# A fused attention kernel: layer 1's merged values by two levels of Strassen instead of one

## The chip, the core and the metric

The kernel runs on one core of a Trainium2 chip. A core has a matrix engine (TensorE, PE in the profile, with its weight loads shown as PEld), a vector engine (VectorE, DVE), an activation engine (ScalarE, ACT), GpSimd (POOL) and SyncE (SP); the last two issue the kernel's DMAs. Operands live in SBUF, TensorE writes to PSUM. The metric is the device time of the whole program in microseconds (us); less is better.

## What is computed

The input is x of shape (8, 512, 32, 32) in fp32: eight batches of 1024 tokens with 512 channels. Two layers follow each other. All of it is in fp32.

```python
# layer 0, per batch
xn = layer_norm(x_flat)                       # over channels
q, k, v = xn @ Wq.T + bq, xn @ Wk.T + bk, xn @ Wv.T + bv     # 8 heads of 64
attn = softmax(q @ k.T / sqrt(64)); out = attn @ v
x = out @ Wo.T + bo + x_flat
# layer 1, per batch, one head of 512 channels
h = group_norm(x, 32 groups)
q, k, v = wq @ h + bq, wk @ h + bk, wv @ h + bv
attn = softmax(q.T @ k / sqrt(512)); o = v @ attn.T
x = x + wp @ o + bp
```

In layer 1 the kernel folds matrices that follow each other into one. The value projection and the output projection become one matrix `m` (wp times wv), so that the "merged values" are m times h, and attention times merged values is already the layer's output. The merged values, 1024 tokens by 512 channels from 512 channels, are the part that is changed.

## The kernel before

**Strassen products.** Almost every matrix product is cut into 2 x 2 blocks and made by Strassen's scheme in Winograd's form: seven products of half-size blocks in place of eight. The list `STEPS` gives the order. Step 0 multiplies block 11 of the weight by block 11 of the operand, step 1 12 by 21, step 2 the sums S2 and T2, step 3 S1 and T1, step 4 S3 and T3, step 5 S4 and 22, step 6 22 and T4. S sums are made of weight blocks (for the merged values they were saved to DRAM once and are loaded with the blocks), T sums of operand blocks. Steps accumulate into three PSUM banks x, z and y. Between the steps ScalarE copies an intermediate state of a bank out (u1, u2, u4 in `leave`, by `plain_shift`) and VectorE adds a copy and a bank into the result (`out`, line 386). The class `Product` holds such a chain: `multiply` issues the matmuls of one step, `leave` the copies and sums that follow it.

**Two levels.** Some products go one level deeper: the half-size products are made by the same seven steps of quarter-size blocks. Two products that end in the same sum run "in tandem", accumulating into the same banks (`project_mixed` for layer 1's queries, `project_deep` for the next batch's keys and queries). The inner sums of weights come from DRAM (`saved_deep`, `load_deep`), the inner sums of operands are "primes", made by VectorE. The queries of layer 1, `project_mixed`, leave the primes of T1, T2, T3 and 22 of h in the dictionary `h1_deep`, and they stay in SBUF through the scores.

**The order within a batch.** For each batch: layer 0's heads (scores, softmax, values), output projection, group norm, layer 1's queries (`project_mixed`), scores (`Whole.scores`, three pairs of products), then the stage in question: the merged values (`project_v(f"vm{b}", ...)`), then the layer's output (`Whole.values`, tiles named o, the units `o_units`), then the next batch's keys and queries (`project_deep`). TensorE, ScalarE, VectorE and GpSimd run in the order in which the program issues (the `manual_schedule` blocks). Work that is not urgent goes into a queue `side` by `later(...)`. `tick(n)` takes n pieces from its front, and the calls of `tick` are spread by hand over the matmul steps (`pieces`). At the merged values this queue holds the end of layer 1's scores (sums `p<-p,p`, line 1360, exponentials, line 1308), the denominator's sums (line 1412) and the operand sums T1 to T4 of the attention weights (line 1423).

**The merged values before.** `project_v` makes two units, one for each half of the tokens of a block. Each runs the seven steps; each step is four matmuls (two token blocks of 128, two halves of the contraction) with 128 stationary columns (operand h) and 256 moving columns (the weight), by `token_part` (line 490). Each unit has four ScalarE copies of 128x512 and three VectorE sums of 128x512. A result `vm` of 1024 tokens is laid out with the token block outermost.

**The output stage.** The units of `Whole.values` run by `value_part` (line 506): four matmuls of 512 moving columns for each step. Before, they run as: two steps of unit 0, two of unit 1, then the rest of unit 0 with some of unit 1, then the rest of unit 1. The weight sums S1 to S4 of the merged values (line 268) are made by VectorE from `later` queue pieces during this stage. `LayerNorm` of the batch after next also puts its pieces there (`ln.queue()`).

**Buffers.** The pool `big` has 46 tiles of 128x1024 fp32, used in rotation by everything of that size; a DMA into a tile on SyncE's queue waits until the former content's last reader is done, and the DMAs behind it wait too. PSUM has three 128x1024 tiles (`wide_psum`) and two of 128x512 (`bank`).

Of the kernel before, what the change touches and what calls it, by code (L numbers as in the profile page):

```python
# [71 lines left out]
def fast_path(ctx: ExitStack, tc: tile.TileContext, x: bass.AP, vecs: dict, weights: dict, out: bass.AP,  # L72
# [48 lines left out]
    def wide(blk):  # L121
        return blk.rearrange("p a t -> p (a t)")
# [89 lines left out]
    saved_deep = {n: dram.tile([P, 3, 2, 4, P], F32, tag=f"saved_deep_{n}", name=f"saved_deep_{n}") for n in ("k", "q", "a")}  # L212
# [289 lines left out]
    def value_part(r):  # L502

        def part(dst, a, b, opens):
            for m in range(NM // 2):
                nc.tensor.matmul(dst, a[:, m, ts(r, P)], b[m // 2][:, m % 2, :], start=(opens and m == 0),  # L506
                                 stop=(m == NM // 2 - 1), skip_group_check=True)
        return part
# [179 lines left out]
    def project_mixed(tag, w, w_deep, bias, h, primes, between, away, beside, ready):  # L688
# [121 lines left out]
        return {(1, 0): m6}, closing  # L810

# [451 lines left out]
    class Whole:  # L1263
# [204 lines left out]
        def values(self, v):  # L1468
            b = self.b
            more = b + 1 < B  # L1470
            w = {f"{i + 1}{j + 1}": v[i, j].rearrange("p (m o) -> p m o", o=CB) for i in range(2) for j in range(2)}
            shared = {}

            def unit(r):
# [25 lines left out]
                def halves(u):  # L1500
# [9 lines left out]
                    for cols in both:  # L1510
                        for m in range(NM // 2):
                            nc.tensor.matmul(u.x[:, cols], w[a][:, m, ts(r, P)],
                                             self.p[b_][m // 2][:, m % 2, cols], start=False,
                                             stop=(m == NM // 2 - 1), skip_group_check=True)
# [12 lines left out]
            for n in SUM_NAMES:  # L1527
                sum_later(w, n, lambda n: big_tile(f"{n}_vm_{b}").rearrange("p (m o) -> p m o", o=CB), wide)
# [18 lines left out]
    with tc.manual_schedule(engines=ORDERED):  # L1547
# [66 lines left out]
        save_deep_later("a", wa, (1, 2))  # L1614
        units, vts = project_v("v0", wv_now, hb)
# [5 lines left out]
        for b in range(B):  # L1621
# [144 lines left out]
            wm_now = load_w("m", b)  # L1766
            next(steps)
            next(steps)
            whole.operands("T2", "T3", "T4")
            v_units, vm = project_v(f"vm{b}", wm_now, h1b)  # L1770
            for u, pieces in zip(v_units, ((2, 2, 2, 2, 1, 1, 1), (1, 1, 1, 2, 1, 2, 2))):
                for u.pieces in pieces:
                    u.step(1)
# [6 lines left out]
            o_units[0].step(2)  # L1780
            if ln:
                ln.queue()
            o_units[1].step(2)
# [20 lines left out]
            if more:  # L1804
                h_deep = {}
                deep_operands_later(hb, h_deep, [n for _, names in TANDEMS for n in names])
# [401 lines left out]
```

## Time and profile before

| | |
|---|---|
| median of 3 runs | 2800.3 us (2799.87 to 2800.49) |
| the profiled execution, its own time | 2798.97 us |
| its span (first to last instruction) | 2797.2 us |
| VectorE busy | 2095.1 us (75%) |
| ScalarE busy | 1248.2 us (45%) |
| GpSimd busy | 527.6 us (19%) |
| HBM read, written | 198.21 MB, 63.44 MB |
| granted clock of TensorE | 1.000 (mean) |

The profile is one execution seen by the hardware's profiler. Groups of instructions are shown as line, engine, operation, output <- inputs with buffer numbers left out, shape, count | busy time, mean duration in ns | idle time of the engine just before them. Each fp32 matmul of the program appears as two records, each with its own weight load: the 56 matmuls that make one batch's merged values stand as 112 records, 896 for the eight batches. Busy time of overlapping records is not counted twice. The start of the merged values of the eight batches lies at 348.1, 689.2, 1030.3, 1371.6, 1712.7, 2053.8, 2394.8 and 2718.4 us. The third, at 1030.27 us, is the one looked at closely.

### The profile page before, as it was taken

Reading aid. Unit: us, or ns where it says so; the run is one execution under the profiler, and the core shown is the slowest. Engines: PE = TensorE matmul, PEld = TensorE weight load, DVE = VectorE, ACT = ScalarE, POOL = GpSimd, SP = SyncE. Lnnn points to the kernel's source line nnn. Section 1 sums busy time; section 2 is a strip of 40 time slices with the busy share of each in tenths; the row PEclk is TensorE's granted clock in tenths of the full one; section 3 lists DMA queues with packets and bytes.
Section 4 is the critical chain, followed back from the end, with each engine's and each line's share of the span. In section 5 each row is a group of like instructions: output and inputs, shape, how many; then the busy total and the mean of one; then the engine's idle time right before and its main releaser. Section 6 shows DMA issues by size and latency. Waiting matters only on the chain.

```text
span 2797.2 us, 31704 instructions
## 1 busy us (share of the span) xinstructions
PE 2786.4 (100%) x10959; PEld 1625.5 (58%) x10959; DVE 2095.1 (75%) x2978; ACT 1248.2 (45%) x2114; POOL 527.6 (19%) x724
## 2 busy tenths in 40 slices
PE   9999999999999999999999999999999999999999
PEld 4535756358553685536854467644676347663375
DVE  6677877778777777777867777678867778657775
ACT  4463425724257242662436533365334733336341
POOL 2031022210222102221122211222112210122001
PEclk9999999999999999999999999999999999999999
DMA  8244367353763547536474364744548433382224
GB/s 318 92 97 125 110 163 191 68 151 110 166 164 70 169 107 181 129 78 188 108 183 107 91 184 108 201 79 117 151 113 208 101 95 117 71 208 63 66 79 99
DMA packets 141018, 365.56 MB, mean 131 GB/s; under 512 B 19776, under 2 KB 24176, under 8 KB 140848
## 3 DMA queue, kind: packets, MB, share of 16 engines
q0 software_dynamic: 58992, 144.22, 27.7%
q1 hardware_dynamic: 81760, 219.19, 22.7%
q8 instruction: 89, 1.46, 0.2%
q14 instruction: 81, 0.66, 0.1%
q10 hardware_dynamic: 96, 0.02, 0.0%
HBM read 198.21 MB, written 63.44 MB: 94 GB/s over the span
## 4 chain that ended last, share of the span: by engine, by line
PE 99%; DMA 0%; DVE 0%; ACT 0%; issue 0%; SPq 0%; DVEq 0%
PE s L1154 16%; PE acc L1172 16%; PE x_o L506 8%; PE s L1320 7%; PE x_v L490 4%; PE x_vm L490 4%; PE y_o L506 4%; PE x_out L481 4%; PE y_s L1320 3%; PE y_v L490 2%; PE y_vm L490 2%; PE s L1355 2%; PE y_out L481 2%; PE z_o L506 2%; PE x_q L604 2%; PE x_k L604 2%
## 5 line engine op out<-in xcount | busy, mean ns | idle before, releaser
L1163 DVE TENSOR_TENSOR sum<-sum,p 128x1024 f32<-128x1024 f32 x384 | 470.3, 1225 | 39.4 <-DVE sum L1163 0.9
L1157 ACT ACTIVATE p<-s 128x1024 f32<-128x1024 f32 (+1 forms) x608 | 478.8, 992 | 15.1 <-PE s L1154 15.1
L1172 PE MATMUL acc<-p,v_again 128*64 128x512 f32 x1792 | 390.9, 594 | 0.0
L1172 PEld LDWEIGHTS acc<-p,v_again 128*64 128x64 f32 x1792 | 126.1, 137 | 261.4 <-issue 236.7
L861 POOL DMA_DIRECT2D fold<-sum x312 | 207.7, 760 | 301.8 <-DMA sum<-sum 174.8
L1154 PE MATMUL s<-q,k 64*128 64x512 f32 x1152 | 252.1, 592 | 0.0
L1154 PE MATMUL s<-q_lower,k_lower 64*128 64x512 f32 x896 | 196.1, 592 | 0.0
L1161 DVE TENSOR_TENSOR sum<-p,p 128x1024 f32<-128x1024 f32 x64 | 78.1, 1220 | 153.0 <-ACT p L1157 153.0
L1154 PEld LDWEIGHTS s<-q,k 64*128 64x128 f32 x1152 | 109.7, 186 | 138.2 <-issue 84.9
L1154 PEld LDWEIGHTS s<-q_lower,k_lower 64*128 64x128 f32 x896 | 85.4, 186 | 110.5 <-issue 68.5
L865 POOL DMA_DIRECT2D sum<-sum x78 | 63.5, 814 | 456.2 <-DVE sum L1163 253.1
L1176 ACT COPY o<-acc 128x512 f32<-128x512 f32 x63 | 36.9, 585 | 221.7 <-PE acc L1172 221.5
L1360 DVE TENSOR_TENSOR p<-p,p 128x1024 f32<-128x1024 f32 x96 | 114.1, 1215 | 6.3 <-ACT p L511 6.3
L506 PE MATMUL x_o<-T_p,S_vm 128*128 128x512 f32 x256 | 114.0, 592 | 0.0
L511 ACT COPY u(0, 0)_v<-x_v 128x512 f32<-128x512 f32 x16 | 9.4, 585 | 186.5 <-PE x_v L490 186.5
L1416 POOL DMA_DIRECT2D sum<-p x32 | 28.0, 925 | 334.6 <-ACT p L1308 240.8
L490 PE MATMUL x_vm<-w_m,T_gn 128*128 128x256 f32 x384 | 90.7, 379 | 0.0
L481 PE MATMUL x_out<-T_o,w_o 128*128 128x512 f32 x192 | 89.2, 594 | 0.0
L506 PEld LDWEIGHTS x_o<-T_p,S_vm 128*128 128x128 f32 x256 | 48.6, 190 | 60.7 <-issue 60.5
L1218 ACT COPY rr<-r 32x16 f32<-32x16 f32 x256 | 53.7, 210 | 62.0 <-DVE r L1121 58.6
L490 PE MATMUL x_v<-w_v,T_h 128*128 128x256 f32 x336 | 80.0, 381 | 0.0
L490 PEld LDWEIGHTS x_vm<-w_m,T_gn 128*128 128x128 f32 x384 | 72.9, 190 | 10.0
(621 smaller groups left out, 5455.7 us busy)
## 6 DMA issues: line engine op xcount, KB each, us to landing
sum<-sum POOLq DMA_DIRECT2D x78, 256.0 KB, 3.4
fold<-sum POOLq DMA_DIRECT2D x312, 64.0 KB, 2.4
x<-in_x_dram SPq DMA_DIRECT2D x32, 512.0 KB, 4.7
xr<-in_x_dram SPq DMA_DIRECT2D x64, 256.0 KB, 4.7
x_away<-x SPq DMA_DIRECT2D x32, 512.0 KB, 3.2
sum<-p POOLq DMA_DIRECT2D x32, 512.0 KB, 5.8
v_away<-v SPq DMA_DIRECT2D x28, 512.0 KB
v_again<-v_away SPq DMA_DIRECT2D x28, 512.0 KB, 7.9
```

The lines of the kernel that those rows point to most:

```text
L481: nc.tensor.matmul(dst, a[:, k, ts(r, P)], b[:, k, :], start=(opens and k == 0), stop=(k == 1), skip_group_check=True)
L490: nc.tensor.matmul(dst[:, ts(m, CB)], b[:, k, ts(2 * r + m, P)], a[:, k, :], start=(opens and m == 0 and k == 0), stop=(k == 1), skip_grou ...
L506: nc.tensor.matmul(dst, a[:, m, ts(r, P)], b[m // 2][:, m % 2, :], start=(opens and m == 0), stop=(m == NM // 2 - 1), skip_group_check=True)
L604: nc.tensor.matmul(dst[:, ts(s, CB)], a[s], b[s], start=(opens and s == 0), stop=True, skip_group_check=True)
L861: nc.gpsimd.dma_start(out=f[ts(q + i, BL), :], in_=t[ts(n, BL), ts(i, HB)], accum_op=ALU.add if n else ALU.bypass)
L1154: nc.tensor.matmul(parts[i], self.k[m // 4][r, ts(m % 4, P)], self.q[r, :], start=True, stop=True)
L1157: nc.scalar.activation(dst, src, AF.Exp, scale=1.0 / float(D) ** 0.5)
L1161: nc.vector.tensor_add(self.sum, self.p[0], p)
L1163: nc.vector.tensor_add(self.sum, self.sum, p)
L1172: nc.tensor.matmul(acc[i * D : (i + 1) * D, :], value_of(self.vt, m, self.c * P + i * D, D), self.p[m][:, ts(i, HB)], start=(m == 0), stop ...
L1320: nc.tensor.matmul(dst[:, ts(c, CB)], x[0][:, ts(c, P)], a[0], start=(opens and c == 0), stop=True, skip_group_check=True)
L1360: nc.vector.tensor_add(wide(t), wide(t), wide(x))
```

## The change

The merged values are made by a new function, `project_values`. Three of Strassen's seven outer products (m1 = 11 by 11, m2 = 12 by 21, m6 = 22 by T4) are made whole: eight matmuls of 256 moving columns each, into the three wide PSUM tiles, and copied out by ScalarE (`evict`, 128x1024). The other four run as two tandems by a second level: unit B takes (S2 by T2) and (S3 by T3), unit C takes (S1 by T1) and (S4 by 22). Each unit has seven inner steps of four matmuls with 128 stationary and 128 moving columns. The inner operand sums are those that the queries left in `h1_deep`; the inner weight sums are saved once at the start (`save_deep_later("m", ...)`, eight small VectorE sums and two DMAs) and loaded for each batch (`load_deep("m", b, (1, 2))`, two DMAs of 512 KB on SyncE's queue, right after the four of the blocks and in front of the next x). The outer results are then put together: m2 += m1 by an accumulating DMA on GpSimd's queue, and twelve VectorE sums of 128x512 (`add` in `project_values`), some of them in the `side` queue.

The results are laid out with the channel half outermost, so `value_part` and the last batch's `halves` read them by `a[:, r, ts(m, P)]`. The sums T3 and T4 of the attention weights are queued behind S2 and S4 of the merged values (in `Whole.values`), and so in the output stage, whose units take their pieces as 5, 1 and 3, 2. The first two of the next batch's inner operands (11 and T2 of h) are made earlier in the output stage, from the same stage's queue.

```diff
--- before.py
+++ after.py
@@ -209,7 +209,7 @@
             nc.sync.dma_start(out=t, in_=d)
         return w
 
-    saved_deep = {n: dram.tile([P, 3, 2, 4, P], F32, tag=f"saved_deep_{n}", name=f"saved_deep_{n}") for n in ("k", "q", "a")}
+    saved_deep = {n: dram.tile([P, 3, 2, 4, P], F32, tag=f"saved_deep_{n}", name=f"saved_deep_{n}") for n in ("k", "q", "a", "m")}
 
     def deep_tile(n, b, g):
         return big_tile(f"w_{n}_{b}_{g}_deep").rearrange("p (s i o) -> p s i o", s=2, i=4)
@@ -503,7 +503,7 @@
 
         def part(dst, a, b, opens):
             for m in range(NM // 2):
-                nc.tensor.matmul(dst, a[:, m, ts(r, P)], b[m // 2][:, m % 2, :], start=(opens and m == 0),
+                nc.tensor.matmul(dst, a[:, r, ts(m, P)], b[m // 2][:, m % 2, :], start=(opens and m == 0),
                                  stop=(m == NM // 2 - 1), skip_group_check=True)
         return part
 
@@ -809,6 +809,112 @@
         q21, q22 = (block(f"{tag}_{n}") for n in ("21", "22"))
         return {(1, 0): m6}, closing
 
+    def project_values(tag, w, w_deep, h, deep):
+
+
+        n_blocks = {n: block(f"{tag}_{n}") for n in ("m1", "m2", "m6")}
+        banks = {n: wide_psum(f"{n}_{tag}") for n in "cba"}
+        made = [[None, None], [None, None]]
+
+        def products(n, t, pairs):
+            a, x = {"m1": ("11", "11"), "m2": ("12", "21"), "m6": ("22", "T4")}[n]
+            for r in pairs:
+                for m in range(2):
+                    for k in range(2):
+                        nc.tensor.matmul(banks[t][:, r * HB + m * CB : r * HB + (m + 1) * CB], h[x][:, k, ts(2 * r + m, P)],
+                                         w[a][:, k, :], start=(k == 0 and m == 0), stop=(k == 1),
+                                         skip_group_check=True)
+
+        def evict(n, t):
+            nc.scalar.copy(n_blocks[n].rearrange("p r (m o) -> p r m o", o=P),
+                           banks[t].rearrange("p (m r o) -> p r m o", r=2, o=P))
+
+        def part(dst, a, x, opens):
+            for s in range(2):
+                for m in range(2):
+                    nc.tensor.matmul(dst[:, ts(2 * s + m, P)], x[s][:, ts(m, P)], a[s],
+                                     start=(opens and s == 0 and m == 0), stop=True, skip_group_check=True)
+
+        def unit(j):
+            def dest(i, k):
+                if made[j][i] is None:
+                    made[j][i] = big_tile(f"{tag}_{j}{i}").rearrange("p (s t) -> p s t", s=2)
+                return made[j][i][:, :, ts(k, CB)]
+
+            def bank_of(to):
+                if to == "y":
+                    return bank(f"y_{tag}_{j}")
+                return banks["c"][:, ts(j, HB)] if to == "z" else banks["ab"[j]][:, :HB]
+
+            a, x = ((("S2", "S3"), ("T2", "T3")), (("S1", "S4"), ("T1", "22")))[j]
+            u = Product(f"{tag}_{j}", weight_inner(w, w_deep, a), operand_inner(h, deep, x), part, plain_shift,
+                        dest, bank_of)
+            u.view = lambda t: t.rearrange("p (s t) -> p s t", s=2)
+            return u
+
+        def step(u, n=1):
+            u.multiply()
+            tick(n)
+            u.leave()
+
+        def add(dst, l, src):
+            nc.vector.tensor_add(dst, l, src)
+
+        def both(work):
+            for r in range(2):
+                work(r)
+
+        m1, m2, m6 = (n_blocks[n] for n in ("m1", "m2", "m6"))
+        products("m1", "c", (0, 1))
+        tick(2)
+        evict("m1", "c")
+        B, C_ = unit(0), unit(1)
+        products("m2", "b", (0, 1))
+        tick(2)
+        evict("m2", "b")
+        step(B)
+        step(B)
+        nc.gpsimd.dma_start(out=wide(m2), in_=wide(m1), accum_op=ALU.add)
+        step(B)
+        step(C_)
+        step(B)
+        step(C_)
+        step(B)
+        step(C_)
+        step(B)
+        products("m6", "c", (0,))
+        tick(1)
+        step(B)
+        step(C_)
+        mb, mc = made
+        both(lambda r: add(mb[r][:, 0], mb[r][:, 0], m1[:, r]))
+        step(C_)
+        products("m6", "c", (1,))
+        both(lambda r: add(mb[r][:, 1], mb[r][:, 1], mb[r][:, 0]))
+        evict("m6", "c")
+        step(C_)
+        c12, c22 = (block(f"{tag}_{n}") for n in ("c12", "c22"))
+        res = {"11": m2}
+
+        def ready(n, t, work):
+            both(work)
+            res[n] = t
+
+        def first_sums(r):
+            add(mb[r][:, 0], mb[r][:, 0], mc[r][:, 0])
+            add(c12[:, r], mc[r][:, 1], mb[r][:, 0])
+
+        later(lambda: first_sums(0), lambda: ready("21", m6, lambda r: add(m6[:, r], m6[:, r], mb[r][:, 1])))
+        step(C_, 1)
+
+        def last_sums():
+            first_sums(1)
+            res["12"] = c12
+
+        side.insert(0, last_sums)
+        later(lambda: ready("22", c22, lambda r: add(c22[:, r], mc[r][:, 0], mb[r][:, 1])))
+        return res
+
     def rows_of(t, c, k):
 
         return t[c][:, k, :] if c in t else t[c // 2, k][:, c % 2, :]
@@ -1465,10 +1571,9 @@
             rows()
             yield
 
-        def values(self, v):
+        def values(self, w):
             b = self.b
             more = b + 1 < B
-            w = {f"{i + 1}{j + 1}": v[i, j].rearrange("p (m o) -> p m o", o=CB) for i in range(2) for j in range(2)}
             shared = {}
 
             def unit(r):
@@ -1509,7 +1614,7 @@
                     both = (slice(0, HB // 2), slice(HB // 2, HB))
                     for cols in both:
                         for m in range(NM // 2):
-                            nc.tensor.matmul(u.x[:, cols], w[a][:, m, ts(r, P)],
+                            nc.tensor.matmul(u.x[:, cols], w[a][:, r, ts(m, P)],
                                              self.p[b_][m // 2][:, m % 2, cols], start=False,
                                              stop=(m == NM // 2 - 1), skip_group_check=True)
                     for cols in both:
@@ -1525,7 +1630,10 @@
                 return u
 
             for n in SUM_NAMES:
-                sum_later(w, n, lambda n: big_tile(f"{n}_vm_{b}").rearrange("p (m o) -> p m o", o=CB), wide)
+                sum_later(w, n, lambda n: block(f"{n}_vm_{b}"), wide)
+                if n == "S2":
+                    self.operands("T3")
+            self.operands("T4")
             return [unit(r) for r in range(2)]
 
     def all_checks():
@@ -1612,6 +1720,7 @@
             u.rest()
         save_deep_later("q", wq_now)
         save_deep_later("a", wa, (1, 2))
+        save_deep_later("m", wm, (1, 2))
         units, vts = project_v("v0", wv_now, hb)
         units[0].pieces = 0
         units[0].step(1)
@@ -1764,23 +1873,28 @@
             steps = whole.scores(h1_deep)
             next(steps)
             wm_now = load_w("m", b)
+            wm_deep = load_deep("m", b, (1, 2))
             next(steps)
             next(steps)
-            whole.operands("T2", "T3", "T4")
-            v_units, vm = project_v(f"vm{b}", wm_now, h1b)
-            for u, pieces in zip(v_units, ((2, 2, 2, 2, 1, 1, 1), (1, 1, 1, 2, 1, 2, 2))):
-                for u.pieces in pieces:
-                    u.step(1)
+            whole.operands("T2")
+            vm = project_values(f"vm{b}", wm_now, wm_deep, h1b, h1_deep)
             o_units = whole.values(vm)
             check = iter(()) if more else all_checks()
             for u in o_units:
                 u.hold = True
             if ln:
                 ln.xt = load_x(b + 2)
-            o_units[0].step(2)
+            for o_units[0].pieces in (5, 1):
+                o_units[0].step(1)
             if ln:
                 ln.queue()
-            o_units[1].step(2)
+            for o_units[1].pieces in (3, 2):
+                o_units[1].step(1)
+            if more:
+                h_deep = {}
+                primes_of_h = [n for _, names in TANDEMS for n in names]
+                deep_operands_later(hb, h_deep, primes_of_h[:2])
+                o_units[0].pieces = 2
             inverse = whole.inverse()
             if more:
                 o_units[0].step(1)
@@ -1802,8 +1916,7 @@
             next(check, None)
             o_units[1].step(1)
             if more:
-                h_deep = {}
-                deep_operands_later(hb, h_deep, [n for _, names in TANDEMS for n in names])
+                deep_operands_later(hb, h_deep, primes_of_h[2:])
             o_units[1].rest()
             if more:
                 wq_next = load_w("q", b + 1)
```

## The prediction

> **What bounds the kernel now.** I read the page's shares first, then the chain of work that ended last, then who waited for whom, then the stage itself.
>
> ```profile
> span 2797.2 us, 31704 instructions
> PE 2786.4 (100%) x10959; PEld 1625.5 (58%) x10959; DVE 2095.1 (75%) x2978; ACT 1248.2 (45%) x2114; POOL 527.6 (19%) x724
> ...
> PE 99%; DMA 0%; DVE 0%; ACT 0%; issue 0%; SPq 0%; DVEq 0%
> ```
>
> TensorE is busy for 2786.4 of 2797.2 us, and 99% of the last chain is its own work. A PE "busy" could hide matmuls that stand still, so I compared starts: in the third batch's merged values the 112 records start at even steps.
>
> ```profile
> 1030.27:1054.45 24.18, 24.18 (x114) 21.27 (x113) 20.28 (x21) 10.17 (x14) 4.33 (x5) 1.00 0.73 186
> ...
> 349.83 1.89 PE L490 MATMUL z_vm<-w_m,gn 128*128 128x256 f32 x8
> 351.56 1.89 PE L490 MATMUL x_vm<-w_m,T_gn 128*128 128x256 f32 x8
> ```
>
> The first line is the stage by windows: 24.18 us, PE and then DVE (20.28) and ACT (10.17) busy. The other two are first-batch timeline rows: eight records begin every 1.73 us, 0.216 each, and 112 x 0.216 = 24.19, the whole stage. Nothing else is in it. So one microsecond of matmul streaming taken out is one microsecond gained, unless it exposes a wait; and any wait that is added is paid in full. Eight batches multiply both.
>
> **What the Trainium skill says.** "TensorE: Matmul & The Clock Gate", section Back-to-back issue gap, says that the spacing in a stream of weight loads and matmuls is set by both of them together, so that short matmuls gain less than their columns suggest; section LDWEIGHTS gives a load as columns / 1.2, 107 ns for 128 columns. This decides the case, because the change halves the columns that stream per load. In the trace a load is recorded at 190 ns, and under 256 columns (216) it hides:
>
> ```profile
> L490 PEld LDWEIGHTS x_vm<-w_m,T_gn 128*128 128x128 f32 x384 | 72.9, 190 | 10.0
> ...
> 1.26 3.57 PE L1550 MATMUL ps_first<-ones 128*128 128x128 f32 x15 [1.26 <-DVE checks L142]
> ...
> 4.88 1.08 PE L301 MATMUL pst_q<-ident,w_q 128*128 128x128 f32 x4
> ...
> 6.17 1.53 PE L301 MATMUL pst_q<-ident,w_q 128*128 128x128 f32 x12 [0.20 <-DMA w_q<-in_L_conv_wq_dram]
> ...
> 19.93 1.97 PE L301 MATMUL pst_v<-ident,w_v 128*128 128x128 f32 x16
> ```
>
> With 128 columns there are two kinds of rows, all at the start. Transposes (line 301): their single starts within the last two rows are 0.109 us apart, but their load is recorded at only 140 ns. Real fp32 matmuls (line 1550) have starts 0.213 us apart, at a time when the array ran slowly: the transposes at 4.88 us have 0.213 too ((1.08 - 0.44, one duration) / 3), and the same transposes have 0.109 from 6.2 us on. At equal clock, then, the real matmul with its own full load kept the transposes' pace, although its load was recorded at 333 ns there. I take 0.109 us. Bounds: below, 0.107 (half of 0.213; nothing streams 128 columns faster); above, 0.190, if at full clock a load must finish before the next matmul starts, as its record would have it. The forecast goes by the traces' pace; the rule's "both" enters as the rival below.
>
> **The change, part by part.** *Removed per batch:* 112 records of 256 columns, 24.19 us. *Added:* three whole products, 3 x 8 matmuls = 48 records x 0.216 = 10.37 us; two units of seven steps of four matmuls = 112 records of 128 columns x 0.109 = 12.21 us. Stage: 22.58 us, 1.61 less. Eight batches: -12.9 us. The output stage keeps its matmuls.
>
> *ScalarE in the new stage.* I count from the stage's start. A ScalarE copy begins 0.2 us after its step's last issue and takes 0.586 (128x512) or 1.018 (128x1024, the `qa_m` copy of line 769). m1 ends at 3.46, m2 at 6.91, unit B's steps 0 and 1 at 7.78 and 8.66. The copy of m2 runs 7.11 to about 8.1, u1 of B 8.02 to 8.61; B's step 2 writes the same bank and wants its load one slot ahead, at 8.55. It gets it about 0.05 after the copy, at 8.66: 0.11 us late. The queries' stage has this very pattern (a step of 0.864 us, then the bank again), and pays for it:
>
> ```profile
> 973.24 0.73 PEld L706 LDWEIGHTS a_qa<-T_deep_gn,w_a_deep 128*128 128x128 f32 x4 [0.21 <-ACT u(0, 0)_qa L511]
> ```
>
> There the copy ended at 973.19, the load began at 973.24 and one start came 0.295 after the former in place of 0.216: 0.08 us. I take 0.11 per batch, 0.9 in all; bounds 0 (copy of m2 just in time) and 0.3. The later waits for ScalarE have room: B's step 5 (at 13.9) needs u4 behind two exponentials (1.05 each): 13.7; C's step 4 (18.2) needs a copy done at 16.0; C's step 5 (20.8) one at 19.0.
>
> *VectorE.* Each unit's three sums stay. Added are twelve sums of 128x512, 0.60 each when queued (line 914: 0.684 less the 0.08 overlap of neighbours), 7.2 us per batch. Four sums of 1024 (T3, T4: 1.135 queued) move behind. Who waits: unit C's last step needs one at 21.4, wanted at 21.7. The output's first z step (26.1) needs c12's first half: 24.7. The second z step (33.0) waits, by its shared bank, for the first z's sum, and in front of that sum lie, from the step at which VectorE was last in time (12.9): seven sums of 1024 (8.0), eighteen of 512 (10.8), gaps behind direct dependencies (0.9): it ends at 32.6. Spare: about 0.25 us. Later pieces have microseconds: the output's step 2 (36.4) needs S2 and T2, at 30.8; T3, T4, S3, S4 are done by 38.3 and wanted from 46.7 on. So I cost these at nothing; if VectorE is later by more than 0.25, the rest is paid once per batch. The first inner sums of keys, moved forward, take 1.5 us out of the time in front of the keys, where block 22's sums ended 0.2 us before use (1107.06 against 1107.26).
>
> *Queues.* m2 += m1 is issued by GpSimd at about 8.4 us; like transfers landed 5.8 us later, and it is wanted at 22.6. It stands in front of the denominator's four transfers, which start later (12.3 on). The two inner weight loads wait for the queries' weights (their tiles) and are issued near 987; the windows show a DMA share of 0.39 until 1015 and 0.00 to 1030. They are wanted at 8.6 and 13 us of the stage. On SyncE's queue the next x goes behind tiles that come free 7 to 15 us into the stage, in place of 0 to 7; VectorE first touches it near 47. The eight inner weight sums at the start run beside the first values, whose matmuls never wait. All nothing; uncovered, a late x would cost a wait of its delay once per batch.
>
> Sum: -12.9 + 0.9 = -12.0 us. The profiled execution of 2798.97 (1.8 around its span) would be 2787.0, its span 2785.2. The median is 1.3 above that execution, so I forecast 2788.3 us.
>
> **Rivals.**
> *The load decides (slower).* Place: the 112 short records per batch. If the spacing is 0.190, each costs 0.081 more: 112 x 0.081 x 8 = 73 us, 2861. It decides from (24.19 - 10.37) / 112 = 0.123 us on: beyond that the kernel is slower than before. For it: the skill's rule, and the 190 ns record is longer than the streaming. Against it: the equal pace at the slow clock, and transposes spaced 0.109 under 140 ns loads, so a record's tail doesn't hold up the next.
> *VectorE is late.* If each of the 25 sums between 12.9 and 32.6 takes 0.04 more, z waits 1.0 - 0.25 = 0.75 us per batch: +6, 2794. For it: 20.28 of 24.18 us busy already and twelve sums more. Against: the old output stage left VectorE idle for 2 to 4 us several times, which takes up what comes later.
> *Transfers hold the next keys and queries.* The windows 1102 to 1127 show a DMA share of 1.02. If their weights land at a fixed time, the 1.6 us come back as waits: 2800. Against: no PE wait is seen there, and these transfers are issued on events that move forward with TensorE.
>
> **How the numbers follow.** Forecast 0.70 (2786.5 to 2791: stall 0 to 0.5 per batch, pace 0.107 to 0.111); VectorE late or a pace of 0.112 to 0.12: 0.10, around 2794; transfers 0.06, around 2800; load decides 0.14. The range 2786 to 2796 takes the first two. 0.2% is 5.6 us, about what a measurement can tell from no change. Faster by more: 0.70 and over half of the second, 0.76; within: 0.10; slower: 0.14.
>
> **What would show it.** PE records of line 835 starting 0.109 apart; the stage 22.7 us long; one short wait per batch for u(0, 0); PE still 100% busy. Wrong if those starts lie 0.12 or more apart, if the second z step waits for VectorE, or if keys wait for weights.

## The result, and the profile after

The changed kernel takes 2817.22 us (median of 6 runs, 2810.71 to 2820.89), the kernel before 2800.09 us (2799.72 to 2800.49). The ratio is 1.0058, with a 95% interval of 1.0043 to 1.0073: slower by 17 us where 12 us less was forecast, and outside the range of 2786 to 2796. The profiled execution took 2820.89 us, with a span of 2819.2.

The page of the changed kernel, its first lines and the shares of the chain that ended last:

```profile
span 2819.2 us, 32630 instructions
PE 2788.4 (99%) x11343; PEld 1630.4 (58%) x11343; DVE 2157.5 (77%) x3082; ACT 1272.0 (45%) x2138; POOL 535.3 (19%) x734
...
PE 77%; DMA 9%; issue 9%; DVE 4%; POOL 1%; ACT 1%; DVEq 0%; POOLq 0%; SPq 0%; ACTq 0%
```

PE's share of the span says 99% where it said 100%, which looks harmless. The chain says more: TensorE's own work was 99% of it and is 77% now, and DMA and VectorE stand in it. The view of waits, TensorE's own, names the places (total us, times, longest):

```profile
PE x_o L506 <- DVE u(1, 1)_o L386: 14.8, 6, 3.5
PE s L1461 <- DVE p L386: 4.0, 6, 0.8
```

Neither wait is in the kernel before. Both occur six times, in the batches 1 to 6. The first is in the output stage, behind the changed one; the second is in the scores, ahead of it. The changed stage itself does nearly what was forecast (third batch, by windows, whose columns are length, busy PE, PEld, DVE, ACT and POOL, then the granted clock, the DMA share and GB/s; then its timeline):

```profile
1039.55:1062.49 22.94, 22.94 (x162) 21.70 (x161) 20.50 (x23) 13.11 (x17) 3.48 (x4) 1.00 0.63 156
...
1046.46 1.05 PE L835 MATMUL a_vm<-w_m,T_gn 128*128 128x128 f32 x8
1047.35 1.06 PE L835 MATMUL c_vm<-w_m,T_gn 128*128 128x128 f32 x8
```

22.94 us in place of 24.18, and eight short records start every 0.89 us, 0.112 us apart. So where did the 22.0 us by which the span grew come from? I summed the distances from one matmul record's start to the next, line by line, in both traces:

| where | us |
|---|---|
| merged values, 8 stages | -9.9 |
| output, line 506: six waits | +15.8 |
| output, line 506: matmuls at a lower clock behind four of these waits | +6.6 |
| scores of layer 1 (lines 1426 and 1461) | +6.3 |
| before the first values (by 24 us of the span) | +1.5 |
| behind the last matmul | +1.4 |
| sum | +21.7 |

The third row is seen where a wait was long. The second batch, by windows:

```profile
745.00:747.50 2.50, 2.50 (x7) 0.88 (x5) 2.31 (x4) 2.36 (x12) 0.00 (x0) 1.00 0.01 3
747.50:750.00 2.50, 0.17 (x1) 0.00 (x0) 2.50 (x4) 0.84 (x3) 1.66 (x2) 1.00 0.06 4
750.00:752.50 2.50, 1.29 (x2) 0.77 (x3) 2.43 (x5) 0.00 (x0) 0.27 (x2) 0.65 0.87 134
752.50:755.00 2.50, 2.50 (x5) 0.99 (x5) 2.47 (x4) 1.87 (x2) 0.77 (x1) 0.67 0.89 199
755.00:757.50 2.50, 2.50 (x8) 1.06 (x7) 2.50 (x3) 1.10 (x2) 0.87 (x1) 1.00 1.02 265
```

TensorE stands still from about 747.7 to 751.2, and the granted clock then falls to 0.65 and 0.67. Records of 512 columns start 0.854 us apart in place of 0.429 until about 754.5, which costs another 1.55 us.

**The wait at x_o.** Step 6 of the output's unit 0 writes the bank that its step 4 filled, so it needs VectorE's sum u(1, 1)_o. VectorE works in its order, and here is what stands in front of that sum in the third batch (its timeline in the changed kernel; in brackets idle time and what ended it):

```profile
1086.21 0.71 DVE L975 STREAM_TRANSPOSE fold1t<-fold 128x512 f32<-128x512 f32 x1 [5.18 <-DMA fold<-sum]
...
1090.47 1.25 DVE L961 STREAM_TRANSPOSE rden<-rr 128x1024 f32<-128x1024 f32 x1 [0.16 <-ACT rr L1561]
1091.75 1.29 DVE L1596 TENSOR_TENSOR u(0, 0)_o<-u(0, 0)_o,rden 128x512 f32<-128x512 f32 x2
...
1094.88 0.68 DVE L386 TENSOR_TENSOR u(1, 1)_o<-u(1, 1)_o,x_o 128x512 f32<-128x512 f32 x1
```

VectorE is not short of time here: it idles 5.18 us, because the transpose of the softmax denominators waits for the transfers that fold them. The sum comes 8.67 us behind that transpose and takes 0.68; TensorE would want it 30.9 us into the output (1062.49 + 30.9 = 1093.4). So the transposed denominators must come within about 21.6 us of the output's start. Here they come at 23.7. In the kernel before they came at 18.4 to 20.8 in these six batches, and its sum u(1, 1)_o started as late as 30.0 in the second: that kernel stood 0.2 us from this wait (30.9 less the sum's 0.68 is 30.2).

**Why the denominators are late.** They are summed by transfers on GpSimd's queue: four `sum<-p` of 512 KB, two `sum<-sum`, eight folds. First the changed kernel's queue in the third batch, then that of the kernel before (its stage started at 1030.27, its output at 1054.45):

```profile
1047.96 0.87 POOL L877 DMA_DIRECT2D vm_m<-vm_m  x1 [33.95 <-ACT vm_m L829]
1052.19 0.87 POOL L1522 DMA_DIRECT2D sum<-p  x1 [3.35 <-ACT p L1414]
1054.57 0.87 POOL L1522 DMA_DIRECT2D sum<-p  x1 [1.51 <-ACT p L1414]
1060.49 0.87 POOL L1522 DMA_DIRECT2D sum<-p  x1 [5.05 <-DMA sum<-p]
1064.65 0.87 POOL L1522 DMA_DIRECT2D sum<-p  x1 [3.30 <-DMA sum<-p]
...
1072.63 0.80 POOL L971 DMA_DIRECT2D sum<-sum  x1 [4.72 <-DMA sum<-p]
...
1082.98 1.61 POOL L967 DMA_DIRECT2D fold<-sum  x2 [3.56 <-DMA fold<-sum]
```

```profile
1039.27 0.87 POOL L1416 DMA_DIRECT2D sum<-p  x1 [33.76 <-ACT p L1308]
1044.39 1.77 POOL L1416 DMA_DIRECT2D sum<-p  x2 [4.25 <-PE x_vm L490]
1049.48 0.87 POOL L1416 DMA_DIRECT2D sum<-p  x1 [3.32 <-issue]
```

The fourth transfer into the sums left 5.0 us ahead of the output's start and now leaves 2.2 us behind it. Two things differ. The first two leave later (12.6 and 15.0 us into the stage in place of 9.0 and 14.1); both now wait for ScalarE's exponentials. And the transfers have more company: SyncE's queue in the changed kernel, then in the kernel before:

```profile
1046.65 8.03 SPq L155 DMA_DIRECT2D x<-in_x_dram  x4
1062.68 18.04 SPq L209 DMA_DIRECT2D w_k<-saved_k  x3
```

```profile
1030.46 7.46 SPq L155 DMA_DIRECT2D x<-in_x_dram  x4
1047.73 3.77 SPq L209 DMA_DIRECT2D w_k<-saved_k  x3
```

The load of the next x (4 x 512 KB) was issued in the first 7 us of the stage, ahead of the sums. It now goes out 7 to 15 us into the stage, together with them, and the load of the next keys' weights behind it on SyncE's queue meets the halvings and folds. In the third batch the four sums took 8.0, 9.5, 6.1 and 7.7 us to land. Over the whole execution the median of a `sum<-p` was 7.8 us where it was 5.8. The kernel before was not free of this: there the third and fourth sum met the keys' weights and took 7.9 and 11.7 us, but they had started early enough. The seventh batch has no next-but-one x to load, but it has the keys' weights, issued from 1.2 us ahead of the output to 1.7 us behind its start: there the transposed denominators come at 19.6, and TensorE doesn't wait.

### The profile page after: what moved, and what is told of

Same layout as the page of the kernel before. It is cut to its first block, busy times and chain, and to the rows that moved or that the text cites. A ratio compares the mean times of both kernels' runs of the same rounds, so it can differ in the third digit from the quotient of the medians.

```text
span 2819.2 us, 32630 instructions
## 1 busy us (share of the span) xinstructions
PE 2788.4 (99%) x11343; PEld 1630.4 (58%) x11343; DVE 2157.5 (77%) x3082; ACT 1272.0 (45%) x2138; POOL 535.3 (19%) x734
## 4 chain that ended last, share of the span: by engine, by line
PE 77%; DMA 9%; issue 9%; DVE 4%; POOL 1%; ACT 1%; DVEq 0%; POOLq 0%; SPq 0%; ACTq 0%
PE s L1260 16%; PE acc L1278 16%; PE x_o L506 4%; PE x_v L490 4%; PE x_out L481 3%; PE s L1426 3%; DMA sum<-p 3%; PE y_o L506 2%; DMA fold<-sum 2%; PE x_k L604 2%; PE x_q L604 2%; PE y_v L490 2%; PE y_out L481 2%; DMA sum<-sum 1%; PE c_qa L698 1%
## 5 line engine op out<-in xcount | busy, mean ns | idle before, releaser
L506 PE MATMUL x_o<-T_p,vm_c 128*128 128x512 f32 x120 | 60.8, 654 | 14.8 <-DVE u(1, 1)_o L386 14.8
L490 PEld LDWEIGHTS x_v<-w_v,T_h 128*128 128x128 f32 x336 | 63.3, 190 | 11.3 <-issue 3.3
L1461 PE MATMUL s<-qa,T_gn 128*128 128x512 f32 x128 | 60.9, 598 | 4.0 <-DVE p L386 4.0
```

The source lines that it names most:

```text
L490: nc.tensor.matmul(dst[:, ts(m, CB)], b[:, k, ts(2 * r + m, P)], a[:, k, :], start=(opens and m == 0 and k == 0), stop=(k == 1), skip_grou ...
L506: nc.tensor.matmul(dst, a[:, r, ts(m, P)], b[m // 2][:, m % 2, :], start=(opens and m == 0), stop=(m == NM // 2 - 1), skip_group_check=True)
```

## The experiments

The theories: **A**, the denominators come late by way of their transfers, and the sum stands behind them in VectorE's order; within it, A1 (the exponentials fell behind), A2 (the transfer m2 += m1 or the transfers' own slowness), C (other loads take the DMA engines). **B**, the rival: the moved sums give VectorE too much to do. **T2**: the wait in the scores comes from the new loads of inner weights. Each kernel below was measured beside the kernel before, whose medians lay at 2800.1 to 2800.6 us. The changed kernel has the six runs above, which lie 10 us apart, so a total that is a few us below its median shows little by itself.

**1. Only the moves** (`moves_only`): the kernel before, with T3, T4 and the first inner sums in the output stage.

```diff
-            whole.operands("T2", "T3", "T4")
+            whole.operands("T2")
...
+                if n == "S2":
+                    self.operands("T3")
+            self.operands("T4")
...
+                deep_operands_later(hb, h_deep, primes_of_h[:2])
```

> The kernel before, with only the moves made: T3, T4 and the first inner sums of the next keys' operand in the output stage; merged values as before. Theory A: the exponentials and the denominators' transfers keep their places, no wait at x_o, total 2799 to 2802. Rival B (the moves make VectorE late): waits at x_o<-T_p,vm of 1 us or more in six batches, total 2807 or more.

2801.24 us, ratio 1.0002 (0.9994 to 1.0011), and no wait at x_o. The moves cost nothing that can be told from zero (TensorE waits once, 1.2 us, for a load of the queries' inner weights). In this kernel the x load went out earlier still (from 2.4 us ahead of the stage in the third batch), and the transposed denominators came at 16.3 to 18.0.

**2. The first inner sums put back** (`primes_back`).

```diff
-                deep_operands_later(hb, h_deep, primes_of_h[:2])
...
-                deep_operands_later(hb, h_deep, primes_of_h[2:])
+                deep_operands_later(hb, h_deep, primes_of_h)
```

> The changed kernel, with the first inner sums of the next keys' operand put back where they were (behind the output's step). Theory A: the transposed denominators still come 5 us late against the output's start, only some 0.85 us of sums leaves the way of u(1,1)_o, so the six waits at x_o<-T_p,vm_c shrink from 2.4-3.7 to 1.5-2.9 us; total 5 to 10 us less than the changed kernel. Rival B (the moved sums make VectorE late): the waits go, total near 2795.

2837.98 us, ratio 1.0142 (1.0125 to 1.0159): worse, which neither theory had said. The denominators came as late as in the changed kernel (22.7 to 25.8), but the sum followed 10.9 us behind them in place of 8.67. A step's side work is taken from a queue: with the inner sums gone from it, four pieces of the layer norm (`x<-x,mu`, 1.2 us each) moved up in front of the sum. B falls by this and by the first run; the effect of taking a piece out was not to shorten the order but to let the next piece in.

**3. The loads of inner weights later** (`late_load`).

```diff
-            wm_deep = load_deep("m", b, (1, 2))
             next(steps)
+            wm_deep = load_deep("m", b, (1, 2))
             next(steps)
```

> The changed kernel, with the two loads of the merged weights' inner parts issued one third of the scores stage later. Theory T2 (these loads share the DMA engines with the queries' closing transfer qa<-qa, VectorE stands 1.9 us for it, and TensorE waits 0.8 to 0.9 us at s<-qa): these waits go in all six batches, the closing sum starts where it did before the change, total 5 to 6 us less than the changed kernel. Rival (VectorE is late at s<-qa for another reason, such as the next layer norm): the waits stay, no change of the total beyond 1 us.

2811.75 us, ratio 1.0041 (1.0028 to 1.0054): 5.5 us less than the changed kernel by the medians, though the two kernels' runs overlap (2805.82 to 2816.45 here). No wait at s<-qa is left. VectorE's timeline in the first batch shows the closing sum that stood for a transfer, in the changed kernel and then in this one:

```profile
314.03 0.75 DVE L756 SCALAR_TENSOR_TENSOR qa<-qa,ua,qa 128x512 f32<-128x512 f32 x1 [1.88 <-DMA qa<-qa]
```

```profile
312.34 0.74 DVE L756 SCALAR_TENSOR_TENSOR qa<-qa,ua,qa 128x512 f32<-128x512 f32 x1
```

The bracket of 1.88 us is gone. In the changed kernel the two loads were issued at 305.81 and 306.65, just ahead of the queries' closing transfer, which took 5.9 us to land; it took 3.8 before the change and takes 3.8 in this kernel. T2 stands, and the combinations below give its price.

**4. The row of denominators one step later** (`late_rows`).

```diff
             o_units[0 if not more else 1].step(1)
-            next(inverse)
-            for u in o_units:
-                u.hold = False
-                u.finish()
             if more:
                 wk_next = load_w("k", b + 1)
                 wk_deep = load_deep("k", b + 1)
             for u in o_units:
                 u.pieces = 2
+            if more:
+                o_units[0].step(1)
+            next(inverse)
+            for u in o_units:
+                u.hold = False
+                u.finish()
             o_units[0].rest()
```

> The changed kernel, with the step that turns the denominators into a row (and the products with it) put behind one more matmul step, so that the sum u(1,1)_o no longer queues behind it on VectorE. Theory A (the denominators come late, and the sum that frees the output's bank stands behind them in VectorE's order): the six waits of 2.4 to 3.7 us at x_o<-T_p,vm_c go, with the slow-clock records behind them; line 506 loses about 22 us, total 2793 to 2797. Rival B (VectorE has simply too much work in the output stage): the wait shrinks by less than 1 us per batch or moves to the next step, total 2810 or more.

2851.65 us, ratio 1.0181 (1.0164 to 1.0198), a clear miss. The edit did two things, and the second was not thought of: the loads of the next keys' weights are no longer behind the row. SyncE's queue and VectorE's wait in the third batch:

```profile
1075.32 19.88 SPq L209 DMA_DIRECT2D w_k<-saved_k  x4
1095.29 1.34 SPq L221 DMA_DIRECT2D w_k_deep<-saved_deep_k  x3
```

```profile
1103.34 0.71 DVE L975 STREAM_TRANSPOSE fold1t<-fold 128x512 f32<-128x512 f32 x1 [9.23 <-DMA fold<-sum]
```

Four more loads went out from 1095 on, when the last two folds were issued (1095.34), and these folds, 64 KB each, took 5.8 and 7.4 us to arrive; the median of a fold in this execution is 2.4. The row also was the wrong part to move: the transpose that waits for the folds was left in front of the sum. The miss pointed at theory C.

**5. The sum ahead of the denominators' row** (`sum_first`): inversion, copies and row each one step later, and no side piece at the step that the sum belongs to.

```diff
             if more:
+                o_units[0].step(2)
+                next(inverse)
+                o_units[1].step(1)
+                next(inverse)
+                o_units[0].pieces = 0
                 o_units[0].step(1)
-            next(inverse)
-            next(check, None)
-            o_units[0].step(1)
-            next(inverse)
-            o_units[0 if not more else 1].step(1)
+            else:
...
             next(inverse)
```

> The changed kernel, with the inversion, the copies and the row of denominators each one matmul step later, no side piece ahead of the sum u(1,1)_o, and the loads of the next keys' weights left behind the row. Theory A: the denominators come as late as before (the transposed fold near 23.7 us of the output stage), but u(1,1)_o is summed near 27.7 to 28 us, ahead of its need at 30.9: the six waits at x_o<-T_p,vm_c and the slow-clock records go, total 2792 to 2797. Rival B (too much work on VectorE): a wait of 1 us or more comes up in the steps behind, or at the next keys; total 2803 or more.

2800.38 us, ratio 1.0001 (0.9992 to 1.001): 16.8 us less than the changed kernel. The denominators came as late as ever (23.2 to 23.9), the sum started at 27.7 in each of the six batches, and no wait at x_o is left. The total is 3 us above the expectation: the waits in the scores stayed and grew a little (4.2 and 1.5 us).

**6. The exponentials earlier** (`early_exp`).

```diff
         products("m1", "c", (0, 1))
-        tick(2)
+        tick(3)
...
         products("m2", "b", (0, 1))
-        tick(2)
+        tick(3)
         evict("m2", "b")
-        step(B)
+        step(B, 0)
```

> The changed kernel, with three side pieces in place of two behind m1 and behind m2, and none at unit B's first step, so that the exponentials of p21 come some 2.6 us earlier. Theory A1 (the denominators are late because these exponentials fell behind, and with them the four transfers into the sums): the first transfer is issued near 10 us of the stage in place of 12.6, the transposed fold comes 1 to 2.6 us earlier, the wait at x_o shrinks by as much, total 2800 to 2810. Rival A2 (the transfers themselves are slow, whatever their start): the fold comes at the same time, total within 3 us of the changed kernel.

2816.32 us, ratio 1.0067 (1.0049 to 1.0085), no change that can be told from the changed kernel. The first transfer left only 0.9 us earlier, and the third, which waits for the first two to land, left no earlier. The edit moved less than the 2.6 us that were meant, so it tests A1 weakly; run 8 settles it.

**7. Without the transfer m2 += m1** (`no_m2m1`): this kernel leaves the sum out, so its block 11 of the merged values is m2 alone.

```diff
-        nc.gpsimd.dma_start(out=wide(m2), in_=wide(m1), accum_op=ALU.add)
```

> The changed kernel without the transfer that adds m1 to m2 (block 11 of the merged values is then m2 alone). Theory A2 (this transfer of 512 KB stands in front of the denominators' and takes their place on the DMA engines): the third and fourth transfers into the sums come 1 to 2 us earlier, the waits at x_o shrink by as much, total 2803 to 2811. Theory A1: the first two transfers wait for ScalarE and are issued at the same 12.6 and 15.0 us, and the total stays within 4 us of the changed kernel.

2813.61 us, ratio 1.0055 (1.0038 to 1.0071). The transposed denominators came at 22.6 to 25.4, as in the changed kernel (23.4 to 25.2); the waits at x_o add up to 12.8 us (14.8 there), and the total lies inside that kernel's own spread. This transfer isn't the cause.

**8. The x load held back** (`late_x`): GpSimd writes eight columns of each x tile behind its last fold, and the load waits for that.

```diff
+                if behind_folds:
+                    nc.gpsimd.memset(t[j, k][:, 0, :8], 0.0)
                 nc.sync.dma_start(out=t[j, k], in_=...)
...
-                ln.xt = load_x(b + 2)
+                ln.xt = load_x(b + 2, True)
```

> The changed kernel, with the load of the next-but-one x held behind the last fold of the denominators (GpSimd first writes eight columns of each x tile, and the load waits for that). Theory C (the x load, which moved from 0-7 us of the stage to 7-15, and the load of the next keys' weights behind it on SyncE's queue take the DMA engines from the denominators' transfers): the third and fourth transfers are issued near 5.5 and 2.4 us ahead of the output stage, as in the seventh batch, which has no x load, in place of 2 ahead and 2 behind; the transposed fold comes 4 to 8 us earlier, no wait at x_o, total 2792 to 2798. Rival A2 (each transfer is slow by itself or for its start): the fold moves by less than 1.5 us, the waits stay, total 2812 to 2820; a late x could also make the layer norm wait (total above 2820).

2800.15 us, ratio 1.0001 (0.9992 to 1.001). GpSimd's queue in the third batch (output from 1054.97 on):

```profile
1044.69 0.87 POOL L1524 DMA_DIRECT2D sum<-p  x1 [3.36 <-ACT p L1416]
1047.06 0.87 POOL L1524 DMA_DIRECT2D sum<-p  x1 [1.51 <-ACT p L1416]
1049.52 0.87 POOL L1524 DMA_DIRECT2D sum<-p  x1 [1.58 <-DMA sum<-p]
1052.58 0.87 POOL L1524 DMA_DIRECT2D sum<-p  x1 [2.19 <-DMA sum<-p]
...
1066.07 1.61 POOL L969 DMA_DIRECT2D fold<-sum  x2 [1.43 <-DMA fold<-sum]
```

The first two transfers leave where they did (12.6 and 15.0 us into the stage), the fourth 4.6 us earlier, and the last folds at 11.1 us of the output in place of 20.5. The four sums took 4.6, 5.0, 5.3 and 5.1 us to land. No wait at x_o is left, although the exponentials are as late as in the changed kernel: A1 alone doesn't make the wait. The total is 2 us above the expectation, again by the scores (4.0 and 1.8 us of waits). On SyncE's queue the keys' weights stand behind the x load, so this edit also holds them back (x from 1067.82 on, the weights from 1070.94); hence the next run.

**9. Only the keys' weights held back** (`late_wk`): the same write on the tiles of `load_w("k", ...)`, the x load left where the change put it.

```diff
+            if n == "k":
+                nc.gpsimd.memset(t[:, 0, 0, :8], 0.0)
             nc.sync.dma_start(out=t, in_=d)
```

> The changed kernel, with only the loads of the next keys' weights held behind the last fold (GpSimd first writes eight columns of each tile); the x load stays where the change put it. Theory C1 (the x load alone makes the denominators late): the third and fourth transfers stay near 2 us ahead of and 2 us behind the output's start, the transposed fold stays above 21.7 us, waits at x_o of 1 us or more remain, total 2805 to 2818. Theory C2 (the weights' loads, which meet the halvings and folds, do it as much): the four transfers stay late, but the halvings and folds behind them run in 8 to 9 us as in late_x, the transposed fold comes near 15 to 20 us, no wait at x_o, total 2799 to 2803.

2800.53 us, ratio 0.9999 (0.999 to 1.0008). The four sums still leave late (the fourth 1.7 to 3.1 us behind the output's start), but what follows is faster. In the third batch:

```profile
1055.73 0.87 POOL L1524 DMA_DIRECT2D sum<-p  x1 [2.75 <-DMA sum<-p]
...
1060.61 0.80 POOL L973 DMA_DIRECT2D sum<-sum  x1 [1.42 <-DMA sum<-p]
```

The second halving leaves 4.9 us behind the fourth sum; in the changed kernel it left 8.0 us behind it (1064.65 to 1072.63). The fourth sum took 4.6 us to land in place of 7.7, while the first two, with the x load beside them, took 8.1 and 9.1. The transposed denominators come at 19.4 to 21.9, and the only wait at x_o is 0.2 us, in the batch with 21.9. The bound of 21.6 us worked out above is met from both sides.

So each load does its part: the x load slows the first sums, the keys' weights the last sum and the folds. Holding back the keys' weights alone is enough. Holding back the x load alone was not run, since run 8 holds both; the seventh batch of the changed kernel, with the keys' weights and no x load, speaks for its being enough too.

**10. Combinations.** `late_x_load` has the edits of 3 and 8, `x_load_sum` those of 3, 5 and 8, `all_three` those of 3, 5 and 6.

> The same hold of the x load, and the merged weights' inner parts loaded a third of the scores stage later. Theories C and T2 together: neither the waits at x_o nor those at s<-qa are left, eight stages of 22.94 us in place of 24.18 (9.9 us) are gained in full, total 2788 to 2792. If a cause is missing, there is a wait of 0.5 us or more per batch somewhere, total 2794 or more.

> The kernel of late_x_load, with the sum u(1,1)_o also ahead of the denominators. Under theory C the denominators are no longer late, so this adds nothing: total within 2 us of late_x_load. If the x load was not the whole cause, this one is 3 us or more faster than late_x_load.

> The changed kernel with the three edits together: the inner weights loaded later, the exponentials earlier, and the sum u(1,1)_o ahead of the denominators. Theory A with T2: no wait at x_o and none at s<-qa, only the 0.07 us at unit B's third step; eight stages of 1.24 us saved, total 2788 to 2792, faster than the kernel before. Rival B: a new wait of 1 us or more per batch, total 2800 or more.

| kernel | us | ratio to before (95%) |
|---|---|---|
| late_x_load | 2791.66 (2791.39 to 2792.53) | 0.9971 (0.996 to 0.9982) |
| x_load_sum | 2791.76 (2790.63 to 2792.17) | 0.9968 (0.9957 to 0.998) |
| all_three | 2793.19 (2791.02 to 2796.44) | 0.9973 (0.9962 to 0.9984) |

All three are faster than the kernel before, by 0.3%, and each interval ends below 1; all_three is 1.2 us above its expectation. late_x_load differs from late_x by the edit of run 3 alone, and 8.5 us lie between them (2800.15 and 2791.66, with runs that don't overlap): that is the price of T2 with no wait at x_o (the gaps in the scores' matmuls differ by 7.9 us). In late_x_load no wait of TensorE that the change brought is left; page and windows (the stage and its output, third batch):

```profile
PE 2777.7 (100%) x11343; PEld 1629.1 (58%) x11343; DVE 2157.4 (77%) x3082; ACT 1271.4 (46%) x2138; POOL 537.0 (19%) x758
```

```profile
1029.34:1052.28 22.94, 22.94 (x162) 21.70 (x161) 20.49 (x23) 13.12 (x17) 4.35 (x5) 1.00 0.52 99
1052.28:1100.50 48.22, 48.22 (x115) 21.41 (x114) 42.52 (x64) 11.87 (x29) 14.15 (x22) 1.00 0.78 205
```

VectorE has as much to do as in the changed kernel (42.52 us busy in the output; 42.59 there, in a stage that a wait had stretched to 50.39 us), and TensorE doesn't stand: the amount of VectorE's work was never the matter. Two of the six batches of all_three have a wait of 1.6 us at y_o for a ScalarE copy; the totals of the three kernels are too close to rank them. Once the denominators came in time, the sum's place no longer mattered, as x_load_sum shows.

## Why the prediction was wrong

*The pace (right in kind, a little small).* Forecast 0.109 us, measured 0.1117 on average, under loads recorded at 192 ns. The rule of the Trainium skill ("TensorE: Matmul & The Clock Gate", section Back-to-back issue gap) that a load and its matmul set the spacing together didn't hurt here: the records' tails overlap, and 0.123, the point from which the rival "the load decides" would have decided, was not reached. 112 x 0.0027 x 8 = 2.4 us of the forecast gain are lost by it.

*The stall at unit B's third step (right).* One gap of 0.18 us in place of 0.112 in each of the eight batches: 0.07, forecast 0.11.

*VectorE in the new stage and the second z step (right).* The z step starts in its turn, at 1072.79; the 25 sums fit. Keys and queries wait for nothing, so the rival "transfers hold the next keys and queries" is wrong as well.

*"Queues ... All nothing" (the step that failed).* The forecast saw most of the facts: that the transfer m2 += m1 stands in front of the denominators' four transfers "which start later (12.3 on)", that the next x goes out "7 to 15 us into the stage, in place of 0 to 7", and that the inner weights are issued near 987 us, which is while the queries close. It did not list that the keys' weights, behind x on SyncE's queue, would move as well. It asked of each moved transfer only who needs its own data, and when. It did not ask who else is on the DMA engines then. The x load's own reader is at 34 us of the output, and it could wait; but with it and the keys' weights in flight the sums and folds came late, and their reader is VectorE, which has a sum for TensorE queued behind. Costed at nothing, these moves were worth +22.4 us in the output and +6.3 in the scores. Of the 22.4 only 15.8 are waits; the other 6.6 are the lower clock behind them, so a wait was paid in more than full.

*"Later pieces have microseconds" (failed too).* I worked out when VectorE would be ready by adding up its instructions. The denominators, which come by DMA, were not in that sum. In the kernel before, the same sum already started at 30.0 us in one batch of six where 30.2 was the last moment; reading the third batch alone (28.0) hid that.

*The rival "VectorE is late"* named the right engine and the wrong reason and place: 6 us for sums that take longer, at the z step. No rival was a transfer that makes another transfer late.

*What of the gain was real.* The stages are worth 9.9 us; late_x_load gets 8.4 of them by its median. What it lacks is in its profile: 1.0 us before 24 us of the span and some 1.4 us behind the start of the last matmul (8.0 us to the end of the span in place of 6.5). Both are in the changed kernel too; their cause wasn't tried.

## What to carry to other kernels

When a change moves a transfer, ask two questions of it: when its own data are wanted, and which other transfers are in flight at its new time and who waits for those. A chain of dependent transfers can be slowed by a bulk load at each link, so its slack should be read in every batch before anything is moved next to it. And in an in-order engine look at what stands behind an instruction that waits for a DMA: if it is something that the bounding engine needs, put it in front.

## What the hardware showed

*Waits cost more than their length.* The six waits at x_o of the changed kernel, as gaps over the usual spacing, were 1.86, 3.71, 2.23, 2.38, 2.99 and 2.66 us. The clock fell with the four of 2.38 us and more, and each fall added 1.55 to 1.76 us. But the length alone doesn't decide. In no_m2m1 waits of 3.95 and 3.04 us left the clock at 1.00, and in early_exp one wait of 2.15 us brought half rate and another of 2.15 us did not. Where the wait lies decides. In the traces of this case every change of the granted clock lies on a grid of 3.41 us, and behind 24 us of the span each fall comes at the end of a grid step. Count a wait as idle from 0.43 us behind the start of the last record to the start of the next. The clock then fell with every wait that filled 66% or more of a step, and with none that filled 55% or less; of the four in between, 58% and one of 59% brought a fall, another of 59% and one of 62% did not. The skill's page "TensorE: Matmul & The Clock Gate", section What's actually happening, tells of a half-rate clock that follows activity in free-running windows of about 3.4 us. The grid and the half rate (0.854 against 0.429 us) agree; the page asks for at least one idle window, and here about two thirds of one was enough. In late_rows, with longer waits, the mean granted clock was 0.991, against 1.000 in late_x_load.

*Bulk loads slow accumulating transfers.* Here are the four `sum<-p` of the third batch in the DMA view (count, size each, median us to landing), in the changed kernel and then in late_x_load, where neither the x load nor the keys' weights are beside them:

```profile
sum<-p POOLq DMA_DIRECT2D x4, 512.0 KB, 7.9
```

```profile
sum<-p POOLq DMA_DIRECT2D x4, 512.0 KB, 5.0
```

The page "DMA: Bandwidth & Descriptors", section Queues, rings and completion order, says that a DMA engine takes turns between the queues that have work; these times fit that, and nothing here shows the turns themselves, or separates the engines from the memory that the transfers share.

*The short matmuls.* 128 moving columns with a fresh load each ran at 0.112 us, 256 at 0.216 and 512 at 0.429: at this size the time still goes with the columns.
